# A decoder layer on one core: the rates at which feed forward is mixed into the attention, and the place of the weight roundings

## The chip, the core and the metric

The kernel runs on one core of a Trainium2 chip. Five engines work on it[...]: PE (matmul), VectorE (DVE), ScalarE (ACT), GpSimd (POOL) and SyncE (SP), which here only issues DMAs. The metric is the device time of one execution in microseconds; lower is better.

## The reference

One decoder layer with layer norms behind the residuals, for x of 2 x 1024 tokens x 256. Self attention has 16 heads of 16 with rotary tables and a causal mask; cross attention goes to 77 context tokens; the feed forward is gated, with two hidden layers of 1024 between.

```python
h = silu(tlin(x, w1_w, w1_s)) * tlin(x, w2_w, w2_s)      # 256 -> 1024
h = gelu(tlin(h, h1_w, h1_s))                            # 1024 -> 1024
h = gelu(tlin(h, h2_w, h2_s))                            # 1024 -> 1024
ffn = tlin(h, w3_w, w3_s)                                # 1024 -> 256
# tlin(x, w, s) = (x @ w.T) * s, w holds few distinct values
x = layernorm(x + attn(x, w_qkv, w_proj))                # causal, rotary
x = layernorm(x + xattn(x, ctx, ctx, mask, ...))         # 77 keys
x = layernorm(x + ffn(x))
```

## The kernel before

The 16 tiles of 128 tokens are taken in five chunks (`CHUNKS`): two chunks of two tiles, then three of four tiles. In the text they are chunks 0 to 4. For each chunk the attention goes through these stages:

- `start` (`project`): tokens are turned, queries, keys and values are projected (tiles `xT`, `pq`, `pv`, `qk_pad`), queries and keys are turned back into `q` and `kT`.
- `top` (`maxima`): for each query tile the scores of all four head groups are computed once, as one set of four or more small products into the two score banks `su` (`scores_bank`; there is one pair of them for everything), and VectorE reduces both banks to maxima (`part`, then `m`). The maxima are written into a spare row of `q`, by `sent` DMAs on SP or by a transposed add.
- `weighted` (`values`): the scores again, keys in the rows now, exponentials on ScalarE (`pr`; half of the tile goes through VectorE first), and products with the values (`po`).
- `rest`: `finish` (division, projection with `wproj`, residual and norm), `cross` (the same for the context, its maxima in `top` and `mx`, then its own `finish`), and for all but the first chunk `prepare`, which makes the two planes of the feed forward's input.

The feed forward of a chunk (`feed_forward_exact`) needs the end of that chunk's `rest`. It is 352 products on PE for a chunk of two tiles after its input is prepared, 384 for one of four tiles: `pg` and `pu` for the gate, `pf` for the two hidden layers, and `pf` again for w3. Its activations are gelu on ScalarE, and each hidden tile is split into an upper plane and a remainder (`split`, a subtract on VectorE or POOL). During `values` the gelus are put off (`behindhand`) until `catch_up`, so that the activation table need not change amid the exponentials.

The order of the work on PE, VectorE and ScalarE is the order of the program (`in_order`). It is made by generators. `beside` takes a step of attention; the number that the step yields is credit, in microseconds of PE that the feed forward may have before the next step; then as many feed-forward products are written as the credit pays for. When the feed forward of the chunks attended so far has run out, `starving[0]` is true, credit is dropped, and the stretch is dry. `together` mixes two generators of attention, `rest(n)` and the next chunk's `start` and `top`: it always takes a step of the one with the smallest sum of yields divided by pace (1.0 and 0.25).

POOL and SP are not bound to the program's order: the tile framework's scheduler places their instructions by their dependencies.

The hidden weights are read from DRAM in 22 slices of 128 x 1024 (`NS`). `survey` reads all of them once in the first part (`w`, `seen`) to find out whether they can be used exactly in one pass; `flag` chooses between two branches, and with these inputs it is the one with `feed_forward_exact`. For that branch each slice is copied from DRAM to DRAM by a DMA on POOL's queue, which rounds it (`rounded`); `half_slices` then loads half slices `wr` on SP's queue, six buffers deep, for every chunk anew. Eight of the roundings (`SOONER`) are issued by the survey's first eight steps, and the other fourteen at the head of the branch.

Of the kernel before, what the change touches and what calls it, by code (L numbers as in the profile page):

```python
# [31 lines left out]
KB = KT * P  # L32
# [3 lines left out]
NS = N12 + 2 * NH + N3  # L36
GATES = 3
SOONER = 8
# [5 lines left out]
def kernel(ctx: ExitStack, tc: tile.TileContext, a: dict, out: bass.AP):  # L44
# [107 lines left out]
    for n, (b, t0, nt) in enumerate(CHUNKS):  # L152
        for i in range(nt):
            xs[b, t0 + i] = residual[(0, 2, 4, 8, 0)[n] + i]

    def load_x(b, t):
        nc.sync.dma_start(xs[b, t], a["x"][b, t * P : (t + 1) * P, :])
# [317 lines left out]
    def maxima(b, t0, n, q):  # L475

        late = None
        for i in range(n):
            cols = slice(i * P, (i + 1) * P)
            spans = spans_of(t0 + i)  # L480
            part = pl.small.tile([P, len(spans), NG, 4], F32, tag="part", name="part", bufs=2)
            for m, (kk, c0, c1) in enumerate(spans):
                diagonal = m == len(spans) - 1
                r = c1 - c0
                gs = 512 // r
                for g0 in range(0, NG, gs):
                    gm = min(gs, NG - g0)
                    su = scores_bank()
                    calls = []
                    if diagonal:  # L490
                        for j in range(4):
                            to = su[j // 2][:, j % 2, :].rearrange("p (g n) -> p g n", g=NG)
                            turned_back = ident_h.unsqueeze(1).to_broadcast([P, NG, P])
                            calls.append(((to, causal[:, :P], turned_back), dict(start=True, stop=False)))
                    for gi in range(gm):
                        for j in range(4):
                            rows = slice(32 * j, 32 * j + 32)
                            calls.append(
                                (
                                    (  # L500
                                        su[j // 2][:, j % 2, gi * r : (gi + 1) * r],
                                        q[rows, g0 + gi, cols],
                                        kT[b, kk][rows, g0 + gi, c0:c1],
                                    ),
                                    dict(start=not diagonal, stop=(not diagonal or gi == gm - 1)),
                                )
                            )
                    tiled(calls)
                    if late and first_part[0]:
                        turned = turned_maxima(late[0])  # L510
                    elif late:
                        sent_maxima(q, *late)
                        late = None
                    largest(part[:, m, g0 : g0 + gm, :].rearrange("p g j -> p j g"), su, gm, r)
                    if late:
                        add_maxima(turned, q, late[1])
                        late = None
                    phase[0] = "maxima"
                    yield (0.8 if first_part[0] else 1.6 if starving[0] else 2.6) * gm * r / KB
            top = maxima_of_heads("m")  # L520
            dve.tensor_reduce(top, part.rearrange("p n g j -> p (g j) n"), AX.X, ALU.max)
            late = top, cols
            phase[0] = "maxima"
            yield 0.3 if i < n - 1 or first_part[0] else 1.6
        add_maxima(turned_maxima(late[0]), q, late[1])
        yield 0.8 if first_part[0] else 1.2
# [152 lines left out]
            nc.sync.dma_start(t, a["wf"][i])  # L679
            yield t  # L680

    def half_slices():

        for i in range(2 * NS):
            t = pl.wffn.tile([P, SLICE // 2], F32R, tag="wr", name="wr")
            half = rounded[i // 2][:, i % 2 * (SLICE // 2) : (i % 2 + 1) * (SLICE // 2)]
            nc.sync.dma_start(t.bitcast(F32), half.bitcast(F32))
            yield t
# [181 lines left out]
        yield 1.0  # L870

    def feed_forward_exact(b, t0, n, alone):
        slices = half_slices()
        N = n * P
        product[0] = step = 0.23 * n / KT
        if (b, t0) not in prepared:
            yield from prepare(b, t0, n)
        planes = prepared[b, t0]

        def layer(name):  # L880
            t = pl.acts.tile([P, 2, FC, N], F32R, tag=name, name=name)
            return SimpleNamespace(planes=(t[:, 0], t[:, 1]), done=set())

        def of_units(w):
            return lambda p, k: (w[k // per][:, k % per, :], now.planes[p][:, k, :])

        now = layer("hid")
        raw = None
        for f in range(FC):
            w = next(slices).rearrange("p (s k n) -> p s k n", s=2, k=KC)  # L890
            pg, pu = (bank(name)[:, :N] for name in ("pg", "pu"))
            sums = [
                (ps, lambda p, k, s=s, w=w: (w[:, s, k, :], planes[p][:, k, :])) for s, ps in ((0, pg), (1, pu))
            ]
            for group in [sums] if f == 0 else [[x] for x in sums]:
                yield from planes_summed(group, KC, step, 0)
            before, raw = raw, gated(pg, pu, None, f)
            if f:
                split(before, now, f - 1)
            if f == 1 and behind_gate:  # L900
                behind_gate.pop()()
        split(raw, now, FC - 1)
        early, per = 6, FC // 2
        for s in (2, 3):
            nxt = layer("hid" if s == 3 else "mid")
            for f0 in (0, 2, 3, 4, 5, 6, 7):
                fs = (0, 1) if f0 == 0 else (f0,)
                sums = []
                for f in fs:
                    w = [next(slices).rearrange("p (k n) -> p k n", k=per) for _ in range(2)]  # L910
                    sums.append((bank("pf")[:, :N], of_units(w)))
                yield from planes_summed(sums, FC, step, early if f0 == 0 else 0, now.done)
                for f, (pf, _) in zip(fs, sums):
                    activated(pf, nxt, s, f)
            now = nxt
        through.add((b, t0))
        w3 = [next(slices).rearrange("p (k n) -> p k n", n=C) for _ in range(2 * N3)]
        mv = pl.small.tile([P, n, 2], F32, tag="mv", name="mv")

        def of_tokens(i):  # L920
            cols = slice(i * P, (i + 1) * P)
            return lambda p, k: (now.planes[p][:, k, cols], w3[k // 2][:, k % 2, :])

        for i0 in (0, *range(2, n)):
            tiles = (0, 1) if i0 == 0 else (i0,)
            sums = [(bank("pf")[:, :C], of_tokens(i)) for i in tiles]
            yield from planes_summed(sums, FC, 0.12, early if i0 == 0 else 0, now.done)
            for i, (pf, _) in zip(tiles, sums):
                summed(pf, xs[b, t0 + i], mv[:, i, :])
                if alone:  # L930
                    written(b, t0 + i, 1, mv[:, i : i + 1, :])
        if not alone:
            behind_gate.append(lambda: written(b, t0, n, mv))

    def survey(flag):

        with ExitStack() as first:
# [11 lines left out]
            for i in range(4):  # L949
                load_slice(i)  # L950
            for i in range(NS):
                if i < SOONER:
                    nc.gpsimd.dma_start(rounded[i], a["wf"][i])
                w = loaded[i]
                low = w.bitcast(U16).rearrange("p (n two) -> p n two", two=2)[..., 0]
                if phase[0] == "values":
# [21 lines left out]
    def together(*streams):  # L978

        live = [[g, pace, 0.0] for g, pace in streams]  # L980
        while live:
            s = min(live, key=lambda s: s[2] / s[1])
            try:
                step = next(s[0])
                s[2] += step
                yield step
            except StopIteration:
                live.remove(s)
# [40 lines left out]
    def weighted(n):  # L1029
        if n == 3:  # L1030

            assert {(0, 0), (0, 2)} <= written_out
            load(4)
        yield from values(*CHUNKS[n], queries_of(n))
# [46 lines left out]
        qk_pads.pop()  # L1081
    other_weights = nc.values_load(flag, min_val=0, max_val=1)

    def beside_each_other(forward, wbufs):
        starving[0] = True
        attended.clear()
        attended.add(0)
        written_out.clear()
        exactly[0] = forward is feed_forward_exact
        if exactly[0]:  # L1090
            for i in range(SOONER, NS):
                nc.gpsimd.dma_start(rounded[i], a["wf"][i])
        with part() as mine, in_order():
            pl.wffn = mine.enter_context(tc.tile_pool(name="wffn", bufs=wbufs))
            pl.acts = mine.enter_context(tc.tile_pool(name="acts", bufs=1))
            last = len(CHUNKS) - 1
            parts = [top(1)]
            for n in range(1, last):
                parts += [weighted(n), together((rest(n), 1.0), (chain(start(n + 1), top(n + 1)), 0.25))]
            parts += [weighted(last), rest(last)]  # L1100
            run(beside(chain(*parts), chain(*(fed(n, forward) for n in range(last + 1)))))

# [88 lines left out]
```

## Time and profile before

| what | value |
|---|---|
| median of 3 runs | 1044.72 us (1041.94 to 1045.3) |
| the profiled execution | 1038.93 us, span 1037.2 us |
| mean granted PE clock | 0.944 |
| busy: PE, DVE, ACT, POOL | 916.3, 546.6, 425.8, 174.7 us |
| DMA | 89.61 MB, mean 86 GB/s |
| ACT table loads | 25, 1283 ns each |
| VectorE reductions of scores, 128 x 1024 | 1215 to 1220 ns each |

The profile is of one execution. "Busy" is the time in which an engine has an instruction in hand; the tenths of the page's part 2 give it for 40 equal slices of the span, some 26 us each. The granted clock is the share of full speed that PE was given. In an engine's rows an `x8` counts records; an fp32 product leaves two records, a product of rounded operands one. Some records of matmuls can be missing.

### The profile page before, as it was taken

The page shows a single profiled execution, that of the slowest core. Times are in us where ns is not written, and L with a number is a line of the kernel's source. Part 1 is how long each engine was busy: PE and PEld are TensorE (multiplying, and loading weights), DVE is VectorE, ACT ScalarE, POOL GpSimd, SP SyncE. Part 2 cuts the span into 40 slices and gives each one's busy share as a digit, 9 for nine tenths or more (in the row PEclk, how much of TensorE's full clock was granted, in tenths as well). Part 3 has the DMA queues.
Part 4 walks back from the last instruction along what each step waited for, and adds up shares of the span by engine and source line. Part 5 has one row for each costly group of instructions (what it writes and reads, how often), then busy time and mean ns, then how long its engine had stood idle before and what let it go on. Part 6 is the DMA issues. An engine that isn't in the chain of part 4 may idle for free.

```text
span 1037.2 us, 16399 instructions
## 1 busy us (share of the span) xinstructions
PE 916.3 (88%) x6537; PEld 560.7 (54%) x6542; DVE 546.6 (53%) x887; ACT 425.8 (41%) x668; POOL 174.7 (17%) x257
## 2 busy tenths in 40 slices
PE   7587688998999888999999978889999998778995
PEld 4344574775774644566642365356664326426884
DVE  4364534446645646865555455676665546356213
ACT  2364237333348114332278821423225783144431
POOL 5020421111321200231210102023221100100001
PEclk9788879899999999899999999989999999778998
DMA  8862861230541200222310010012221001002441
GB/s 271 264 227 99 277 192 61 92 113 22 172 154 42 82 3 1 72 92 82 102 42 21 11 49 5 1 50 93 93 92 61 21 11 36 18 0 92 142 146 52
DMA packets 45109, 89.61 MB, mean 86 GB/s; under 512 B 7128, under 2 KB 12928, under 8 KB 44672
## 3 DMA queue, kind: packets, MB, share of 16 engines
q1 hardware_dynamic: 44047, 76.15, 22.8%
q0 software_dynamic: 704, 11.54, 3.3%
q8 instruction: 54, 0.88, 0.4%
q10 hardware_dynamic: 272, 0.79, 0.2%
q14 instruction: 32, 0.25, 0.1%
HBM read 86.19 MB, written 13.63 MB: 96 GB/s over the span
## 4 chain that ended last, share of the span: by engine, by line
PE 68%; DVE 14%; ACT 5%; issue 2%; DMA 2%; POOL 1%; POOLq 0%; DVEq 0%; ACTq 0%
PE pf L89 25%; PE su L89 20%; PE po L89 6%; PE pm L89 5%; PE pt L89 4%; DVE pr L89 3%; PE pg L89 3%; PE pu L89 3%; ACT pr L89 3%; DVE x L89 2%; DMA wr<-rounded 2%; PE pq L89 2%; DVE top L89 2%; DVE stats L89 1%; DVE part L89 1%
## 5 line engine op out<-in xcount | busy, mean ns | idle before, releaser
L89 DVE TENSOR_REDUCE part<-su 128x2 f32<-128x1024 f32 (+3 forms) x149 | 166.8, 1160 | 93.9 <-PE su L89 93.8
L89 PE MATMUL pf<-mid,wr 128*128 128x512 f32 (+1 forms) x640 | 148.8, 369 | 0.5 <-DVE x L89 0.5
L89 PEld LDWEIGHTS pf<-mid,wr 128*128 128x128 f32 x640 | 105.3, 191 | 57.2 <-issue 41.7
L89 PE MATMUL pf<-hid,wr 128*128 128x512 f32 (+1 forms) x640 | 131.7, 357 | 1.2 <-DVE gate L89 1.2
L89 ACT ACTIVATE raw<-pf,sc 128x512 f32<-128x512 f32 (+1 forms) x71 | 42.3, 606 | 190.4 <-PE pf L89 188.9
L89 PEld LDWEIGHTS pf<-hid,wr 128*128 128x128 f32 x640 | 103.7, 192 | 30.7 <-issue 12.3
L89 ACT ACTIVATE pr<-su 128x1024 f32<-128x1024 f32 (+1 forms) x124 | 96.3, 776 | 53.7 <-PE su L89 50.2
L89 ACT ACTIVATE pr<-pr 128x1024 f32<-128x1024 f32 (+1 forms) x124 | 100.2, 808 | 19.4 <-DVE pr L89 14.8
L89 PE MATMUL su<-q,kT 32*128 32x512 f32 (+3 forms) x832 | 94.8, 514 | 5.4 <-ACT pr L89 4.8
L89 PE MATMUL su<-kT,q 32*128 32x128 f32 (+3 forms) x1152 | 92.2, 416 | 1.6 <-DVE part L89 1.6
L89 PE MATMUL po<-pr,v 128*32 128x512 f32 (+3 forms) x832 | 87.4, 482 | 5.4 <-ACT pr L89 3.2
L89 DVE TENSOR_TENSOR pr<-su,causal 128x512 f32<-128x512 f32 (+1 forms) x64 | 48.5, 757 | 57.4 <-PE su L89 46.2
L89 DVE COPY pr<-su 128x1024 f32<-128x1024 f32 (+1 forms) x40 | 44.7, 1118 | 44.3 <-PE su L89 43.0
L588 POOL TENSOR_SCALAR_AFFINE_SELECT pr<-pr 128x256 f32<-128x256 f32 x64 | 26.5, 414 | 212.9 <-ACT pr L89 212.9
L89 PEld LDWEIGHTS su<-q,kT 32*128 32x128 f32 x832 | 35.0, 186 | 46.4 <-ACT pr L89 41.6
L89 PEld LDWEIGHTS su<-kT,q 32*128 32x128 f32 x1152 | 44.7, 189 | 28.3 <-issue 16.0
L89 PE MATMUL pg<-x,wr 128*128 128x512 f32 (+1 forms) x160 | 45.5, 397 | 8.4 <-DMA wr<-rounded 7.1
L89 PEld LDWEIGHTS po<-pr,v 128*32 128x32 f32 x832 | 18.1, 109 | 60.1 <-ACT pr L89 28.3
L263 POOL TENSOR_SCALAR rstd<-mv 128x4 f32<-128x4 f32 (+2 forms) x18 | 4.0, 231 | 276.0 <-DVE mv L89 276.0
L89 ACT ACTIVATE gate<-pg,sc 128x512 f32<-128x512 f32 (+1 forms) x40 | 24.0, 602 | 58.3 <-PE pg L89 56.4
L89 ACT ACT_TABLE_LOAD x25 | 32.1, 1283 | 36.2 <-PE su L89 26.9
L788 POOL TENSOR_TENSOR mid<-raw,mid 128x512 fp32r<-128x512 f32 (+1 forms) x29 | 29.7, 1033 | 100.0 <-ACT mid L89 97.7
(131 smaller groups left out, 1233.7 us busy)
## 6 DMA issues: line engine op xcount, KB each, us to landing
wr<-rounded SPq DMA_DIRECT2D x220, 256.0 KB
rounded<-in_wf_dram POOLq DMA_DIRECT2D x22, 512.0 KB, 11.3
w<-in_wf_dram SPq DMA_DIRECT2D x22, 512.0 KB
x<-in_x_dram SPq DMA_DIRECT2D x16, 128.0 KB
out_dram<-x SPq DMA_DIRECT2D x16, 128.0 KB
q<-sent SPq DMA_DIRECT2D x80, 2.0 KB
wqkv<-in_w_qkv_dram ACTq DMA_DIRECT2D x1, 768.0 KB
wk<-in_wkT_dram SPq DMA_DIRECT2D x1, 512.0 KB
```

The source lines that it names most:

```text
L89: ins = getattr(self.engine, name)(*args, **kw).ins
L263: nc.gpsimd.tensor_scalar(rstd, mv[:, :, 1], EPS, None, ALU.add)
L588: nc.gpsimd.affine_select(out=half, in_=half, compare_op=ALU.is_ge, fill=0.0, base=0, pattern=[[0, 2], [1, P]], channel_multiplier=-1,)
L788: sub.tensor_tensor(rest, raw, upper.bitcast(F32), ALU.subtract)
```

## The change

Four edits in the generators:

- In `maxima`, the credit of a step is 1.7 for a full step in all chunks but the first part, where it was 2.6 with feed forward at hand and 1.6 without.
- In `together`, a pace is a function that is asked at each step, and a stream's sum is of yields divided by the pace at that moment. The pace of the next chunk's `start` and `top` is 0.6 while the feed forward has run out and 0.25 otherwise.
- In the survey, the first eight roundings are issued in the last eight steps, not the first eight.
- The other fourteen are issued in `half_slices` of the first chunk's feed forward, one before every second half slice, eight slices ahead of it, and no longer at the head of the branch.

```diff
+    def round_slice(i):
+        nc.gpsimd.dma_start(rounded[i], a["wf"][i])
...
     def maxima(b, t0, n, q):
-                    yield (0.8 if first_part[0] else 1.6 if starving[0] else 2.6) * gm * r / KB
+                    yield (0.8 if first_part[0] else 1.7) * gm * r / KB
...
-    def half_slices():
+    def half_slices(rounding):
         for i in range(2 * NS):
+            if rounding and i % 2 == 0 and i // 2 + SOONER < NS:
+                round_slice(i // 2 + SOONER)
             t = pl.wffn.tile([P, SLICE // 2], F32R, tag="wr", name="wr")
...
     def feed_forward_exact(b, t0, n, alone):
-        slices = half_slices()
+        slices = half_slices((b, t0) == CHUNKS[0][:2])
...
     def survey(flag):
             for i in range(NS):
-                if i < SOONER:
-                    nc.gpsimd.dma_start(rounded[i], a["wf"][i])
+                if i >= NS - SOONER:
+                    round_slice(i - (NS - SOONER))
...
     def together(*streams):
         while live:
-            s = min(live, key=lambda s: s[2] / s[1])
+            s = min(live, key=lambda s: s[2])
             try:
                 step = next(s[0])
-                s[2] += step
+                s[2] += step / s[1]()
                 yield step
...
+    def beside_rest():
+        return 0.6 if starving[0] else 0.25
+
     def beside_each_other(forward, wbufs):
-        if exactly[0]:
-            for i in range(SOONER, NS):
-                nc.gpsimd.dma_start(rounded[i], a["wf"][i])
...
-                parts += [weighted(n), together((rest(n), 1.0), (chain(start(n + 1), top(n + 1)), 0.25))]
+                parts += [weighted(n), together((rest(n), lambda: 1.0), (chain(start(n + 1), top(n + 1)), beside_rest))]
```

## The prediction

> **What bounds the kernel now.** I read the page first, then busy time by stage (the windows view, cut at the stage borders that the PE timeline shows), then the timeline of one step in the stages that change.
>
> The page's parts 1 and 2 come first: busy time and share of each engine, and the span in 40 slices.
>
> ```profile
> PE 916.3 (88%) x6537; PEld 560.7 (54%) x6542; DVE 546.6 (53%) x887; ACT 425.8 (41%) x668; POOL 174.7 (17%) x257
> PE   7587688998999888999999978889999998778995
> PEclk9788879899999999899999999989999999778998
> ```
>
> PE is the bound, with 121 us of idle (1037.2 - 916.3). The dips in slices 13 to 15, 24 to 26 and 34 to 36 recur, and the clock dips with two of them. The windows view says where they are (stretch: length, busy time and record count of PE, PEld, DVE, ACT, POOL, then clock).
>
> ```profile
> 357.00:425.50 68.50, 57.72 (x382) 30.11 (x384) 40.74 (x78) 20.34 (x29) 8.79 (x11) 0.93 0.01 1
> 430.00:530.00 100.00, 99.39 (x643) 63.15 (x639) 62.21 (x66) 31.31 (x46) 26.35 (x21) 1.00 0.29 96
> 594.50:619.50 25.00, 20.87 (x129) 16.89 (x126) 14.64 (x39) 6.99 (x15) 1.35 (x2) 1.00 0.06 19
> 619.50:686.50 67.00, 55.12 (x375) 28.73 (x375) 40.38 (x80) 19.69 (x28) 10.33 (x13) 0.95 0.05 14
> 690.00:795.50 105.50, 104.89 (x671) 66.32 (x670) 67.21 (x73) 32.60 (x48) 26.92 (x21) 1.00 0.29 96
> 860.00:879.80 19.80, 16.80 (x107) 14.07 (x107) 12.17 (x34) 5.40 (x11) 1.27 (x2) 1.00 0.07 21
> 879.80:941.90 62.10, 45.54 (x295) 22.57 (x296) 28.66 (x64) 14.31 (x18) 5.50 (x8) 0.78 0.05 16
> ```
>
> 430:530 and 690:795.5 are the maxima of chunks 3 and 4, beside feed forward: PE has no idle time at all. 357:425.5, 619.5:686.5 and 879.8:941.9 are the cross attentions of chunks 2, 3 and 4 after the feed forward has run dry: 10.8 + 11.9 + 16.6 us idle, and in the last a clock of 0.78. So feed forward is spent where PE was full anyway, and missing where PE waits. One step of the maxima (timeline, chunk 4) says how much room those stages have on the other engines.
>
> ```profile
> 732.64 1.14 PE L89 MATMUL su<-kT,q 32*128 32x512 f32 x8
> 733.71 2.79 PE L89 MATMUL pf<-hid,wr 128*128 128x512 f32 x11
> 733.82 2.35 DVE L89 TENSOR_REDUCE part<-su 128x2 f32<-128x1024 f32 x2 [1.70 <-PE su L89]
> ...
> 736.43 1.14 PE L89 MATMUL su<-kT,q 32*128 32x512 f32 x8
> ```
>
> A step is 3.79 us: scores 1.07, eleven products 2.72 (0.247 each). VectorE reads both score banks for 2.35 us and is through at 736.17, 0.26 us before PE writes them again. There is one pair of score banks, so this is all the slack the maxima have.
>
> **The change, part by part.** Counting feed-forward products in the order of both programs, stage by stage (maxima / values / finish, cross and the next chunk's start):
> chunk 1: 158/45/149 before, 112/45/195 after; chunk 2: 250/37/65, then 166/37/149; chunk 3: 284/36/64, then 163/37/184; chunk 4: 284/36/64, then 187/36/161. The total is the same. The tail (the last chunk's feed forward, 941.9 to 1037.2) is untouched. Prices: 0.247 us at 512 columns (chunks 3, 4), 0.13 at 256 (chunks 1, 2: 17 in 2.2 us), 0.123 for w3 (64 in 7.83 us).
>
> Maxima of chunk 4: 97 products leave, 24.0 us. But with 7.4 products (1.83 us) a step asks 2.90 us of PE, while the banks are busy 1.07 + 2.35 = 3.42. PE can refill the first bank while VectorE reads the second, so the step lies between 2.90 (nothing lost) and 3.45 (nothing overlapped). Following two steps by hand, every second one finds its second bank 0.5 us late: I take 3.15, 0.25 above PE's own time, over some 22 steps 6 us. Behind such a wait on PE stand the next products, and behind those ScalarE's and POOL's activations, which have room (32.60 and 26.92 of 105.50 busy). The gate layer adds a VectorE multiply (741 ns) per eight products to steps that already need 2.35: 3 us. The slow start at 683 to 690 (slow clock, 4 us) goes. Sum -24 + 6 + 3 - 4 = -19.
>
> Maxima of chunk 3: 121 products leave (-29.9), five score sets move into chunk 2's dry stretch (-6), waits as above over 17 steps +5, gate +3: -28.
>
> Maxima of chunk 2: 84 products, -10.9, one set moves out -2, new waits +1: -12. Maxima of chunk 1: 46 products, -6.
>
> Finish and cross of chunk 4 (860 to 941.9, 81.9 us): PE's own work at full clock is 16.8 + 45.5 x 0.78 = 52.3, of which 64 w3 products are 8. After: 44.3 + 97 x 0.247 + 64 x 0.123 = 76.1, plus 6 us of waits that stay (16.80 of 19.80 busy in 860:879.8, which had feed forward beside it): 82. So 24 us of products go in for nothing: 0. The cover is VectorE's and ScalarE's latency in this chain and the clock; should it fail, the 24 us come back. The `wr` loads on SP move with their products, into stretches where the DMA engines are 0.05 busy.
>
> Chunk 3 (594.5 to 686.5, 92 us): 20.9 + 55.1 x 0.95 = 73.3, less 8, plus 120 x 0.247 + 64 x 0.123 = 37.5, plus one more set 1.1, plus waits 6: 110, +18.
>
> Chunk 2 (335 to 425.5, 90.5): its products still run out, after the second of four cross maxima. 84 products come in (+10.5), of which some 5 are hidden. The faster pace puts seven score sets of chunk 3 where there were two. They use the same banks and 2.4 us of VectorE each, in the queue of the chain that ends the stretch (its `x` waits are the longest): two us each, +10. Sum +15.5.
>
> Chunk 1's cross: +46 products (5.8), hidden in the 6.5 us idle of 230 to 253 but for 2; one set more, +1.5.
>
> ScalarE: 24 table loads in this branch become 31; 17 subtracts go from POOL (1.28 us) to VectorE (0.69). What matters are round trips inside the values, where a feed-forward layer ends amid exponentials: one before, in chunk 1, three after, in chunks 2, 3 and 4. The one in the trace:
>
> ```profile
> 176.10 1.28 ACT L89 ACT_TABLE_LOAD   x1
> 177.39 1.03 ACT L89 ACTIVATE raw<-raw 128x256 f32<-128x256 f32 x3
> 178.44 1.28 ACT L89 ACT_TABLE_LOAD   x1
> ```
>
> cost PE 2.97 us waiting for `pr`. The Trainium skill ("ScalarE: Activation LUTs", What ACT_TABLE_LOAD costs) speaks against the change here: it gives a switch about 1283 ns for the load and 1380 more for a drain. By the row the activation starts 10 ns after the load's end and the next load as soon after it: no drain. By the row the three trips cost 9 us and the one that goes gives 3: +6. By the page two more switches' drains per trip make it about +11. I take the row; the page stays in the range.
>
> The roundings: the text moves them, the order hardly does. POOL isn't bound to the program's order, and the eight early ones stand in both programs right after the memsets, waiting for nothing: they still start near 11 us (9.5 before), in the first load of the DMA queues. Of the fourteen later ones eleven still stand in a row at the branch; only the last three are each behind one `hid` subtract. So the burst stays that stalls PE for 7.1 us on `wr` near 124 and 131. The subtracts come some 4 us sooner on POOL, freeing gate buffers; one score set more passes before the stall. I take -2, between 0 and -8; were a late rounding to hold SP's queue, `sent` and the weights behind it would wait, but eight slices' lead leaves that at +3 at most.
>
> Sum: -19 - 28 - 12 - 6 + 0 + 18 + 15.5 + 3.5 + 6 - 2 = -24. The profiled execution took 1038.9 us (span 1037.2), 0.6% under the median, 1044.7; -24 makes 1015 of it and 1020 of the median.
>
> **The rivals.**
> (a) Gain as worked out, 1020: chance 0.58.
> (b) The score banks cost less and the cross hides more. For: in chunk 1's cross, with feed forward beside it, PE idles under 1 us from 197 to 231. Without the bank waits (-12), the new gate waits (-3) and the round trips (-6): -45, 1000. Chance 0.16.
> (c) The banks bind fully: 3.45 a step is +0.3 over 40 steps, 12 us, and VectorE's additional work some 5: -8, about 1037. Chance 0.16, a third of it close enough to zero to be called no change.
> (d) Slower: feed forward beside the cross is not hidden but added. Its activations and subtracts stand in order on ScalarE and VectorE ahead of the small operations that the chain waits for (`y`, `x`, `top`). If nothing is hidden, chunk 4 pays 24 instead of 0, chunk 3 30 instead of 18, chunks 1 and 2 9 more: 44 in all, 1064. It turns the sign where less than about 45% is hidden. Against it stands chunk 1's cross, but with half as wide tiles. Chance 0.10.
> (e) The rounding edit does nothing at all: within (a), 2 us.
>
> **How the numbers follow.** Faster by over 0.3% (3 us, about what a measurement of this kernel can tell from no change): (a), (b), two thirds of (c): 0.84. Within: 0.06. Slower: 0.10. The range leaves out (d) and the far end of (b): 998 to 1041.
>
> **What would show it.** Right: no step of the maxima near 3.79 us, but steps of about 2.9 to 3.4 with PE waiting for `part`; PE over 90% busy and the clock near 1 in the cross of chunks 3 and 4; a dry stretch left in chunk 2 alone, ended by VectorE; 32 table loads in the page; PE idle near 105 us. Wrong: the maxima of chunks 3 and 4 shorter by under 30 us together, or the stages of cross 3 and 4 longer by over 40.

## The result and the profile after

| | before | after |
|---|---|---|
| median (range, 4 runs each) | 1043.33 us (1037.93 to 1045.3) | 1058.07 us (1055.06 to 1059.9) |
| ratio, 95% interval | | 1.0147 (1.01 to 1.0193) |
| profiled span | 1037.2 us | 1056.7 us |

The change makes the kernel 1.5% slower; forecast was 2.4% faster. The page of the changed kernel, parts 1 and 2:

```profile
PE 941.8 (89%) x6542; PEld 564.7 (53%) x6542; DVE 555.1 (53%) x905; ACT 433.5 (41%) x671; POOL 160.9 (15%) x244
PE   7587799997989977799999899989999999988995
PEclk9788899999998988799999999988999999999998
```

PE's idle time fell only from 121 to 114.9 us, and its busy time rose by 25 us though it computes the same products. "Busy" contains products at half clock and sets that stand half written while their second bank is being read. The clock's dip in slices 35 to 37 (counted from one) is gone, as forecast. New ones are in slices 15 to 17 and 27 to 28. The stretches of the prediction again, in the windows view (325.5 to 440.9 is chunk 2's finish, cross and dry part; then the maxima of 3, a window that overlaps the first; finish and cross of 3; the maxima of 4; finish and cross of 4 in three pieces):

```profile
325.50:440.90 115.40, 94.74 (x628) 58.85 (x627) 60.43 (x123) 30.18 (x53) 11.36 (x14) 0.91 0.14 45
434.20:526.40 92.20, 90.02 (x525) 49.65 (x525) 65.59 (x73) 27.35 (x37) 17.26 (x14) 0.93 0.21 67
594.50:705.30 110.80, 100.90 (x608) 64.08 (x609) 54.46 (x119) 33.21 (x52) 14.66 (x16) 0.99 0.15 48
709.30:810.60 101.30, 96.95 (x569) 55.24 (x569) 68.93 (x74) 27.51 (x38) 20.10 (x16) 0.93 0.21 69
878.40:898.20 19.80, 19.14 (x93) 14.13 (x94) 12.31 (x31) 7.16 (x13) 2.60 (x4) 1.00 0.25 80
898.20:954.30 56.10, 51.76 (x375) 31.26 (x375) 25.40 (x51) 19.52 (x25) 5.15 (x6) 1.00 0.12 39
954.30:960.60 6.30, 5.17 (x35) 4.00 (x33) 4.58 (x15) 1.18 (x2) 1.27 (x2) 1.00 0.49 158
```

Finish and cross of 3 take 110.8 us against 110 forecast. Those of 4 are filled at full clock and take 82.2 us against 82 forecast, with 76.07 us of PE against 76.1. But chunk 2's stretch and the maxima of 3 together, 325.5 to 526.4, take 200.9 us; before they took 195 (335 to 530), and 182.5 was forecast. Cross 3 and the maxima of 4 together, 594.5 to 810.6, take 216.1 us; before 201, and 200 was forecast.

To compare kernels I cut each trace at VectorE events that all of them have: the last `m` of a chunk ends its maxima, the last `q<-po` its values, the last `rec` its cross ("maxima" of chunks 2 to 4 therefore hold the end of `rest` and the next start as well, and the tail holds the end of the last `rest`). First column: us before; then the forecast's steps, and the difference to before in each profiled execution. The last column is the changed kernel with the old pace beside chunk 2 alone (`pace_not_chunk_2` below).

| stage | before | forecast | after | credit 1.7 alone | pace alone | credit 2.2, new pace | 1.7, old pace beside 2 |
|---|---|---|---|---|---|---|---|
| first part | 101.0 | 0 | -1.2 | +0.5 | +1.6 | -0.7 | -1.9 |
| maxima 1 | 50.3 | -8 | -8.4 | -8.4 | -1.5 | -4.1 | -8.1 |
| values 1 | 34.2 | -3 | -5.0 | -5.0 | +0.7 | -4.5 | -5.0 |
| cross 1 | 55.8 | +3.5 | -0.8 | -0.8 | +2.2 | +0.2 | -0.8 |
| maxima 2 | 58.0 | -12 | +1.0 | +0.3 | -1.4 | -4.4 | +1.0 |
| values 2 | 34.6 | +3 | +3.8 | +3.4 | +0.2 | -0.3 | +3.8 |
| cross 2 | 76.6 | +15.5 | +26.0 | +8.8 | +18.2 | +15.0 | +12.5 |
| maxima 3 | 109.6 | -28 | -19.1 | -8.6 | -12.1 | -15.3 | -11.7 |
| values 3 | 75.2 | +3 | +3.6 | -0.7 | +0.4 | -0.5 | -0.7 |
| cross 3 | 79.7 | +18 | +18.9 | +8.6 | +9.5 | +13.8 | +8.7 |
| maxima 4 | 110.5 | -19 | -3.7 | -11.3 | -5.0 | -12.2 | -13.6 |
| values 4 | 75.1 | +3 | +3.3 | -0.5 | -0.1 | -0.3 | +3.4 |
| cross 4 | 73.0 | 0 | -4.9 | +0.8 | -2.3 | -3.4 | +0.2 |
| tail | 103.5 | 0 | +6.0 | +2.6 | -0.8 | -0.7 | +7.2 |
| span | 1037.2 | -24 | +19.5 | -10.1 | +9.6 | -17.3 | -5.0 |

How far a stage repeats: the changed kernel was profiled twice (the second is `credit_22_late` below), and no stage differs by more than 2.1 us between the two, those from cross 3 to the tail by 0.3 at most.

### The profile page after: what moved, and what is told of

It is laid out like the page before. It is cut to its first block, busy times and chain, and to the rows that moved or that the text cites. A ratio compares the mean times of both kernels' runs of the same rounds, so it can differ in the third digit from the quotient of the medians.

```text
span 1056.7 us, 16404 instructions
## 1 busy us (share of the span) xinstructions
PE 941.8 (89%) x6542; PEld 564.7 (53%) x6542; DVE 555.1 (53%) x905; ACT 433.5 (41%) x671; POOL 160.9 (15%) x244
## 4 chain that ended last, share of the span: by engine, by line
PE 69%; DVE 13%; ACT 5%; issue 3%; DMA 2%; POOL 1%; SPq 0%; POOLq 0%; DVEq 0%; ACTq 0%
PE pf L89 23%; PE su L89 21%; PE po L89 6%; PE pm L89 5%; PE pt L89 5%; ACT pr L89 3%; DVE pr L89 3%; PE pg L89 3%; PE pu L89 3%; DVE part L89 2%; DVE x L89 2%; PE pq L89 2%; DMA wr<-rounded 1%; PE pv L89 1%; DVE stats L89 1%
## 5 line engine op out<-in xcount | busy, mean ns | idle before, releaser
L89 DVE TENSOR_REDUCE part<-su 128x2 f32<-128x1024 f32 (+3 forms) x149 | 166.9, 1160 | 75.1 <-PE su L89 74.7
L89 PE MATMUL pf<-mid,wr 128*128 128x512 f32 (+1 forms) x640 | 168.3, 387 | 1.7 <-PE pf L89 1.0
L89 PE MATMUL pf<-hid,wr 128*128 128x512 f32 (+1 forms) x640 | 141.3, 361 | 0.1
L89 PE MATMUL su<-kT,q 32*128 32x128 f32 (+3 forms) x1152 | 115.0, 432 | 6.4 <-DVE part L89 6.4
L89 PE MATMUL su<-q,kT 32*128 32x512 f32 (+3 forms) x832 | 96.1, 521 | 11.4 <-ACT pr L89 10.7
L89 PEld LDWEIGHTS su<-kT,q 32*128 32x128 f32 x1152 | 53.5, 195 | 46.8 <-issue 26.9
L793 POOL TENSOR_TENSOR hid<-gate,hid 128x256 fp32r<-128x256 f32 (+1 forms) x32 | 32.8, 1028 | 108.4 <-ACT hid L89 108.4
```

Of the source, the lines that this page charges most:

```text
L89: ins = getattr(self.engine, name)(*args, **kw).ins
L793: sub.tensor_tensor(rest, raw, upper.bitcast(F32), ALU.subtract)
```

## The experiments

Every time below is a median; ratios are to the kernel before, run beside it on the same chip.

**The parts alone.** `credit_only` is the hunk of `maxima` on the kernel before, `pace_only` the hunks of the paces (`together`, `beside_rest` and its call), `roundings_only` the rest.

> The kernel before with one part of the change, the credit of 1.7 in the maxima; paces and roundings as before. Theory of the score banks: a step of the maxima cannot go under about 3.45 us (scores 1.07 and both reductions 2.35), so of the products taken out of chunks 3 and 4 only those above that length save time; the rest cost their full time in the cross stages. Then this part alone carries most of the loss: 1048 to 1058 us, with the steps of the maxima of chunk 4 at 3.4 to 3.5 us. Rival, the pace edit is the cause (seven score sets in chunk 2's dry stretch): then the credit alone is worth what was forecast for it, 1015 to 1035 us.

> The kernel before with another part alone, the pace of 0.6 for the next chunk where feed forward is dry. Theory of the score banks: the early score sets lengthen the dry cross of chunks 2 and 3, and each comes out of the maxima at its full step: within 8 us of the kernel before, 1036 to 1052. Rival, the pace edit is the cause: 1053 to 1070 us, the dry stretches of chunks 2 and 3 longer by 10 us or more each than the maxima behind them become shorter.

> The kernel before with only the weight roundings placed as in the change. Both theories, and the order of the instructions: the early eight start with the others in the first load, eleven of the other fourteen stand together at the branch, so 1041 to 1046 us, no change. Rival: the late roundings hold the loads of wr, 1048 us or more, with longer waits of PE for wr between 110 and 160 us.

| run | us | ratio (95%) |
|---|---|---|
| credit_only | 1027.59 | 0.9852 (0.9827 to 0.9876) |
| pace_only | 1048.57 | 1.0051 (1.0028 to 1.0075) |
| roundings_only | 1042.18 | 1.0005 (0.9988 to 1.0021) |

The first theory falls: the credit alone gains 14 us, as its rival said. The roundings do nothing. But the pace alone costs only 7, which was the first theory's answer for it. -14, +7 and 0 make -7; together the parts make +15. Some 22 us belong to neither part, only to the pair. In the stage table the pair's part is "after" less both single columns: next to nothing in cross 2 (-1.0) and cross 3 (+0.8), and +12.6 in maxima 4, +3.9 each in values 3 and 4, +4.2 in the tail, -3.4 in cross 4.

**Another credit.** In the changed kernel 1.7 becomes 2.2, then also 2.0 and 2.4; and 2.2 with the old paces.

```diff
-                    yield (0.8 if first_part[0] else 1.7) * gm * r / KB
+                    yield (0.8 if first_part[0] else 2.2) * gm * r / KB
```

> The changed kernel with a credit of 2.2 in place of 1.7, all else as changed. Theory of the score banks: 9.5 products of 0.247 us and the scores, 1.07, make 3.4 us, just what the banks take anyway, so the maxima of chunks 3 and 4 are as long as with 1.7 (within 3 us each), some 40 products a chunk leave the cross stages, and the total falls by 10 to 16 us to 1042 to 1048. Rival (maxima are bound by PE alone, products cost the same everywhere): each step longer by 0.5 us, maxima of chunks 3 and 4 longer by 8 us each, cross shorter by as much, total within 4 us of the changed kernel, 1054 to 1062.

> The changed kernel with a credit of 2.0 in all maxima. Between 1.7 (1058) and 2.2 (1024). Theory of the overflow: it depends on whether products still stand behind the last cross; 2.0 is 1.3 products a step more than 1.7 over some 20 steps, 26 of the 37 that spill into the tail, so 1026 to 1040. Rival (a smooth optimum of the mixing rate, without a spill): near 1036, halfway on a line.

> The changed kernel with a credit of 2.4. Theory of the score banks: above 2.2 a product costs its full 0.247 us in the maxima again, about 0.9 products a step over some 40 steps of chunks 3 and 4, 9 us, less what the cross gives back: 1026 to 1036. If the gates and waits bind before, 2.4 is no worse than 2.2 (1020 to 1026), and this is the better version.

> The kernel before with a credit of 2.2 alone. Theory of the overflow: with 2.2 no backlog spills, with the new pace or the old, so the pace is worth no more than 5 us here: 1019 to 1029 us (1024 with the new pace). Rival (the pace edit costs its 7 us in any company, as it did on the kernel before): 1015 to 1019 us.

| run | us | ratio (95%) |
|---|---|---|
| credit_20 | 1029.11 | 0.9879 (0.9829 to 0.9929) |
| credit_22 | 1023.96 | 0.9827 (0.9786 to 0.9868) |
| credit_24 | 1034.6 | 0.9916 (0.9879 to 0.9953) |
| credit_22_old_pace | 1029.6 | 0.9876 (0.983 to 0.9923) |

credit_22 beats both kernels; against credit_only and credit_20 the intervals overlap. Both expectations for it missed: 1042 to 1048 and 1054 to 1062. 0.3 us of credit a step, from 1.7 to 2.0, is worth 29 us beside the new pace. With the old paces 1.7 and 2.2 are level (1027.59 and 1029.6, the intervals overlap). So 1.7 isn't past an edge by itself, only beside the new pace; and at 2.2 the new pace costs nothing that can be told (the intervals overlap, the medians even favour it). The page of credit_22:

```profile
PE 914.6 (90%) x6536; PEld 558.3 (55%) x6542; DVE 552.7 (54%) x899; ACT 423.4 (42%) x667; POOL 162.7 (16%) x245
PEclk9698989999999998999999999889999999999998
```

27 us less PE time than in the changed kernel for the same products. Its maxima of chunk 4 (second line) hold 217 feed-forward products by my count, those of the changed kernel (first line) 195, and yet they are 8.5 us shorter, at a clock of 0.97 for 0.92:

```profile
693.83:800.72 106.89, 100.95 (x581) 58.40 (x581) 76.37 (x96) 22.46 (x35) 20.71 (x18) 0.92 0.20 67
```

```profile
674.26:772.61 98.35, 95.01 (x592) 58.26 (x591) 70.43 (x86) 24.38 (x37) 23.44 (x20) 0.97 0.22 73
```

**The score banks.** One step of the maxima of chunk 4 at a credit of 1.7, in the timeline of credit_only:

```profile
745.05 1.86 PE L89 MATMUL pf<-hid,wr 128*128 128x512 f32 x7
745.54 2.33 DVE L89 TENSOR_REDUCE part<-su 128x2 f32<-128x1024 f32 x2
...
746.89 2.26 PE L89 MATMUL su<-kT,q 32*128 32x512 f32 x8
...
748.06 2.36 DVE L89 TENSOR_REDUCE part<-su 128x2 f32<-128x1024 f32 x2 [0.18 <-PE su L89]
749.08 1.88 PE L89 MATMUL pf<-hid,wr 128*128 128x512 f32 x7
750.89 1.14 PE L89 MATMUL su<-kT,q 32*128 32x512 f32 x8
```

The set at 746.89 takes 2.26 us, the next one 1.14. VectorE reads until 745.54 + 2.33 = 747.87; the second half of the set can only start then. The view calls PE busy all this time. From set to set the four full steps of this tile (sets at 743.72, 746.89, 750.89, 754.00 and 757.37) take 3.17, 4.00, 3.11 and 3.37 us, 3.41 in the mean. If VectorE sets this, half as long reductions must show it:

```diff
-        dve.tensor_reduce(to[:, :2], first, AX.X, ALU.max)
-        dve.tensor_reduce(to[:, 2:], other, AX.X, ALU.max)
+        few = r if first_part[0] else r // 2
+        dve.tensor_reduce(to[:, :2], first[..., :few], AX.X, ALU.max)
+        dve.tensor_reduce(to[:, 2:], other[..., :few], AX.X, ALU.max)
```

> The kernel before with the credit of 1.7, and each reduction of scores reads only the first half of its keys (half of the maxima's work on VectorE is left out). Theory of the score banks: at 7.4 products the step (mean 3.4 us) waits for the banks, so with reductions half as long it falls to PE's own 2.9, and the maxima of chunks 3 and 4 (101.0 and 99.2 us) become 8 to 12 us shorter each. Rival (what keeps the steps long is on PE itself): they stay within 3 us.

> The kernel before, credit 2.6, with the same half reductions (half of the maxima's work on VectorE is left out). Theory of the score banks: at 11 products PE is the bound, so the maxima of chunks 3 and 4 (109.6 and 110.5 us) stay within 4 us. Rival (VectorE bounds these steps at either credit): 8 us or more shorter each.

Of both there is one run, 994.14 and 1019.83 us. With credit 1.7 the maxima of 3 and 4 went from 101.0 and 99.2 to 87.4 and 89.0 us, and the step that waited is gone (timeline of credit_only_half_max, 2.88 us from set to set):

```profile
723.72 1.14 PE L89 MATMUL su<-kT,q 32*128 32x512 f32 x8
724.79 1.88 PE L89 MATMUL pf<-hid,wr 128*128 128x512 f32 x7
724.92 1.29 DVE L89 TENSOR_REDUCE part<-su 128x2 f32<-128x512 f32 x2 [1.84 <-PE su L89]
726.60 0.93 PE L89 MATMUL su<-kT,q 32*128 32x384 f32 x8
```

With 2.6 they went from 109.6 and 110.5 to 104.1 and 105.3. That is over the 4 us expected, but the full steps stayed where they were, 3.79 us from set to set with eleven products (timeline of before_half_max):

```profile
713.43 1.14 PE L89 MATMUL su<-kT,q 32*128 32x512 f32 x8
714.50 2.79 PE L89 MATMUL pf<-hid,wr 128*128 128x512 f32 x11
714.60 1.29 DVE L89 TENSOR_REDUCE part<-su 128x2 f32<-128x512 f32 x2 [2.11 <-PE su L89]
717.22 1.14 PE L89 MATMUL su<-kT,q 32*128 32x512 f32 x8
```

About half of its gain lies in the first steps of each maxima, before feed forward is there (2.9 of 5.5 us in chunk 3, 2.5 of 5.2 in chunk 4). The same four full steps in every kernel, by the starts of their sets; "PE's own" is 1.07 us of scores and 0.247 a product:

| kernel | credit | products in four steps | PE's own, us a step | measured, us a step |
|---|---|---|---|---|
| before | 2.6 | 45 | 3.85 | 3.92 |
| before, half reductions | 2.6 | 45 | 3.85 | 3.85 |
| credit_24 | 2.4 | 41 | 3.60 | 3.74 |
| credit_22 | 2.2 | 39 | 3.48 | 3.64 |
| credit_20 | 2.0 | 35 | 3.23 | 3.59 |
| credit_only | 1.7 | 29 | 2.86 | 3.41 |
| after | 1.7 | 30 | 2.92 | 3.54 |
| credit_only, half reductions | 1.7 | 29 | 2.86 | 2.97 |

So a step is PE-bound at 2.6, and at 1.7 it is held up by VectorE. Between them there is no sharp floor: from 45 to 29 products PE is asked for 0.99 us a step less, and the step becomes 0.51 shorter. About half of what is taken out is saved in the maxima, and all of it must be placed elsewhere.

**Which chunks, which pace.** First, 2.2 in chunks 3 and 4 alone. The run credit_22_late compared a pair of numbers with triples, so it was the changed kernel once more: 1062.01 us, which says how far a repeat goes (1058.07 the first time). credit_22_chunks_3_4 is the edit as meant.

```diff
-                    yield (0.8 if first_part[0] else 1.7) * gm * r / KB
+                    yield (0.8 if first_part[0] else 2.2 if (b, t0, n) in CHUNKS[3:] else 1.7) * gm * r / KB
```

> The changed kernel with a credit of 2.2 in the maxima of chunks 3 and 4 alone, 1.7 in those of chunks 1 and 2. Theory of the overflow: what spills past cross 3 and cross 4 goes (16 and 37 products), the maxima of chunk 3 and 4 stay within 4 us of the changed kernel's or shorter, so most of the loss to the 2.2 kernel comes back: 1026 to 1036 us. Rival (the loss starts in chunks 1 and 2 by their spill into chunk 2's start): 1045 us or more.

> The changed kernel with a credit of 2.2 in the maxima of chunks 3 and 4, 1.7 in those of chunks 1 and 2. Theory: the spill past cross 3 and cross 4 is decided in the maxima of chunks 3 and 4, so it goes, with the trips in their values: 1028 to 1038 us. Rival (the backlog starts in chunks 1 and 2, whose spill into the start of chunk 2 sets the rest): 1045 us or more.

1034.25 us, ratio 0.9899 (0.9863 to 0.9934): of the 34 us between the changed kernel and credit_22, the credit of chunks 3 and 4 brings 24, and that of chunks 1 and 2 the other 10. Then the pace back at 0.25 beside the rest of one chunk:

```diff
-                ... (chain(start(n + 1), top(n + 1)), beside_rest))]
+                ... (chain(start(n + 1), top(n + 1)), (lambda: 0.25) if n == 2 else beside_rest))]
```

> The changed kernel (credit 1.7), with the pace of the next chunk back at 0.25 beside the rest of chunk 2 alone; beside chunks 1 and 3 it is the changed one. Theory of the overflow: the score sets of chunk 3 that pass in chunk 2's dry cross bring no feed forward with them, since credit is dropped while it is dry; 30 products fewer in the maxima of chunk 3, and the backlog spills past cross 3, into the start of chunk 4 and the tail. Then this one edit undoes the interaction: 1026 to 1034 us, no product of chunk 2's feed forward behind cross 3, maxima of chunk 4 near 99 us (107 in the changed kernel). Rival (each early set costs by itself, wherever it is placed, and chunk 3's stay): half of the loss or less comes back, 1042 us or more.

> The changed kernel with the pace back at 0.25 beside the rest of chunk 1 alone. Theory: feed forward hardly runs dry there with a credit of 1.7, so the new pace does little: 1050 to 1060 us. Rival (chunk 1's pace holds the 11 us that the kernel with the old pace beside chunk 2 still lacks to the credit alone): 1044 to 1049 us.

Beside chunk 2: 1038.56 us, 0.9961 (0.9941 to 0.9981), with single runs from 1033.8 to 1044.1. It is between the two expectations: some 20 of 30 us. Its profile is of one of its fastest runs, 1033.89. Beside chunk 1: 1057.95, nothing. So the pair meets in chunk 2's cross: with the new pace the maxima of chunk 3 hold 24 sets, not 26, and 156 products, not 186. A set that passes while it is dry takes its credit along. The dry stretch, from the last product before it to the first behind it, in the windows view (the changed kernel, then pace_not_chunk_2):

```profile
373.50:444.10 70.60, 52.55 (x321) 24.62 (x320) 44.06 (x78) 15.84 (x21) 4.78 (x6) 0.85 0.02 8
```

```profile
373.10:425.00 51.90, 40.47 (x259) 20.17 (x259) 33.98 (x68) 15.83 (x21) 4.79 (x6) 0.90 0.02 7
```

It begins at the same time (373.5 and 373.1) and holds 6.5 sets against 2.5 (by the reductions in it); at seven or eight products a set, the four more are the 30 that are missing. They lengthen it by 18.7 us. The loss of the pair shows behind it: with the old pace there, values 3 gets back 4.3 us and maxima 4 gets back 9.9.

**Table trips.** In the changed kernel's values a layer of the feed forward ends amid exponentials three times. ScalarE's timeline and PE's, chunk 4:

```profile
806.73 1.28 ACT L89 ACT_TABLE_LOAD   x1
808.02 0.63 ACT L89 ACTIVATE raw<-raw 128x512 f32<-128x512 f32 x1
808.67 1.28 ACT L89 ACT_TABLE_LOAD   x1
809.97 1.02 ACT L89 ACTIVATE pr<-su 128x1024 f32<-128x1024 f32 x1
```

```profile
811.04 1.61 PE L89 MATMUL su<-q,kT 32*128 32x512 f32 x8 [2.61 <-ACT pr L89]
```

```diff
         for layer, f, raw in tiles:
-            act.activation(raw, raw, AF.Gelu)
+            if phase[0] == "values":
+                act.activation(raw, raw, AF.Exp, scale=0.0)
+            else:
+                act.activation(raw, raw, AF.Gelu)
```

> The changed kernel; where put-off gelus are caught up amid exponentials, an exponential of zero is computed in their place (those gelus are left out), so no table is changed there. Theory: each of the three trips in the values costs 3.3 to 4 us of PE's time, so 8 to 13 us go, to 1045 to 1050 us, and the rest of the loss stays in the maxima and the cross. Rival (the trips cause most of the loss): 1038 us or less; other rival (their time is covered): 1055 or more.

1049.16 us, ratio 1.006 (1.004 to 1.008): 9 us less than the changed kernel at first, and 12.9 less than its copy that ran beside this one (credit_22_late, 1062.01). Values 2, 3 and 4 became 4.4, 4.2 and 4.2 us shorter, 12.8 in all. So the trips are 9 to 13 of the 34 us. In chunk 4 the wait is 2.61 of the 4.2; behind it PE runs at half clock from 811.6 to 815.0, which loses 1.7 more, and without the trip it doesn't.

**The spill.** In the changed kernel the feed forward of chunk 3 isn't through when cross 4 ends. PE's timeline there:

```profile
954.31 3.21 PE L89 MATMUL pf<-wr,hid 128*128 128x256 f32 x24
957.80 1.96 PE L89 MATMUL pt<-ident,x 128*128 128x128 f32 x8 [0.28 <-DVE x L89]
```

By my count 37 products stand behind the last `rec`, and 16 behind cross 3. I thought these were the edge that 2.0 avoids. To test it, 64 products are left out, in the changed kernel and in credit_22, where nothing spills:

```diff
-            yield from planes_summed(sums, FC, 0.12, early if i0 == 0 else 0, now.done)
+            yield from planes_summed(sums, FC, 0.12, early if i0 == 0 else 0, now.done, 1 if n == 4 and not alone else 2)
```

(The new last argument is the number of planes, two where it isn't given.)

> The changed kernel; in the feed forward of chunks 2 and 3 the second plane of the w3 products is left out, 32 products each, 64 x 0.123 = 7.9 us of PE's time in all. In the changed kernel 16 and 37 products spill past cross 3 and cross 4. Theory of the spill: without it the maxima of chunk 4 and the tail give back 5 us each beyond the products' own time, 1040 to 1047 us in all. Rival (products cost their own time wherever they are): 1049 to 1052 us.

> The kernel with credit 2.2 and the new pace, and the same 64 products left out; nothing spills there. Theory of the spill: they cost no more than their own time, and part of it is hidden beside the cross, so 3 to 8 us go: 1016 to 1021. Rival (leaving out w3 products shortens a chain of its own): 1013 or less.

1055.49 us, 1.0137 (1.0092 to 1.0182), and 1022.92, 0.9812 (0.978 to 0.9845): 3 and 1 us less, each time less than either expectation had. The theory falls. In the profile the tail gave back 3.3 us for 32 products (3.9 us at 0.123) and the maxima of chunk 4 only 1.8. Spilled products cost at most their own time.

## Why the prediction was wrong

The order of the work was read rightly: by count, 184 products are written from the end of values 3 to the end of that feed forward (168 up to the last `rec`, 16 behind it) and 161 in chunk 4 (124 and 37), as forecast, and 32 tables are loaded. Several stages came out too: cross 3 (+18, measured +18.9), and cross 4 and the last feed forward. The stage table cuts these two at the last `rec` (-4.9 and +6.0); at the forecast's own border, the first gate product of the last feed forward, they are 82.2 us for 82 and 96.1 for 95.3. The forecast's own sign of being wrong held: the maxima of 3 and 4 became 22.8 us shorter together, under 30.

Two sums came out in part by luck. Chunk 1's maxima (-8, -8.4) had 2 us of the roundings in them; `roundings_only` shows +0.1 there, and the credit alone has the -8.4. The trips (+6; three at 3.3 to 3.8 and one fewer at -5.0 make +5.7) were priced at 3 each. The prediction's row showed the loads rightly, with no drain between them, but PE's wait isn't the whole price: a trip takes 4.2 to 4.4 us of its stage.

The sum missed by 43.5 us, from -24 to +19.5. By stage: maxima 4 by 15.3, maxima 2 by 13.0, cross 2 by 10.5, maxima 3 by 8.9. These steps failed:

- **"Two us each, +10."** The largest. Four more early score sets in chunk 2's dry cross made it 18.7 us longer, 4.7 each (the dry stretch of the changed kernel against that with the old pace there). 5.7 of that is half-clock time, 10.8 us against 5.1, which the forecast didn't have; the rest is still over 3 us a set. Taking the new pace away beside chunk 2 alone gives 19.5 us back.
- **"I take 3.15, 0.25 above PE's own time."** With credit alone the quiet step is 3.41, 0.55 above PE's own 2.86; in the changed kernel it is 3.54 (3.47 in chunk 3), over the forecast's upper end of 3.45. The half reductions show the mechanism: 2.97. For 40 steps this is 10 to 15 us. Rival (c) took the full binding but kept the rest of the sum. It doesn't turn the sign by itself: credit_only has it and gains 14 us.
- **Maxima 2, -12, measured +1.0.** Missed: with cross 1 no longer dry, w3 products of chunk 0 follow its end (18 by count), and PE then waits 3.94 us for `qk_pad` at 241 us, where it waited 2.01 before. With 2.2 nothing follows, the wait is 1.21, and the stage gains 4.4. The 18 products are worth 2.2 us at 0.123, PE's idle time in the stage rises by 2.6 and its half-clock time by 1.7. The rest of the 13 us isn't accounted for, and nothing was left out to test it.
- **Maxima 4, -19, measured -3.7.** Credit alone has -11.3. The other 7.6 us stand beside a clock that is lower by nearly as much (half-clock time lost: 8.5 us, against 1.7 in credit_only). VectorE comes into its first steps with the norm of the previous feed forward, and PE, with fewer products in hand, waits:

```profile
721.91 2.35 DVE L89 TENSOR_SCALAR x<-x,mv,rstd 128x256 f32<-128x256 f32 x4
...
724.38 2.33 DVE L89 TENSOR_REDUCE part<-su 128x2 f32<-128x1024 f32 x2
```

```profile
725.73 3.21 PE L89 MATMUL su<-kT,q 32*128 32x512 f32 x8 [2.14 <-DVE part L89]
```

The norm alone doesn't explain it. In credit_only it stands among the first steps as well, and PE waits nearly as long, but the clock stays full:

```profile
696.38 2.32 DVE L89 TENSOR_SCALAR x<-x,mv,rstd 128x256 f32<-128x256 f32 x4
```

```profile
698.93 0.27 PE L89 MATMUL pt<-ident,m 128*16 128x128 f32 x1 [1.95 <-DVE m L89]
```

Rival (d) named almost the time, 1064, for the wrong reason: feed forward beside cross 3 and 4 was hidden as forecast.

What stays open is the pair's 22 us in full. The trips of values 3 and 4 are 8 of them, shown by leaving them out. Most of the rest is maxima 4, 12.6 us: it goes when the new pace beside chunk 2 goes, which is shown. Why it is that long is not: half clock is some 7 of it, and leaving out the 16 products that spill into it gave back only 1.8.

## What to carry to other kernels

Filler beside a stage isn't paid in full or not at all. Count what the slowest other engine needs per step (here 3.4 us, scores and two reductions on one pair of banks) and compare it with PE's own time at several rates: well above it most of a product that is taken out is saved, towards it less (here three quarters from 45 products to 39, under four tenths from 39 to 29), and all of it must be placed elsewhere. Edits that all move filler into one place must be tried together and apart, since each can gain or cost little alone and the pair lose: a credit of 1.7 was as good as 2.2 with the old paces and 34 us worse with the new one. And "PE busy" isn't PE computing: compare the duration of like sets (1.14 and 2.26 us) before believing that an engine is full.

## What the runs showed of the hardware

The granted clock comes in pieces of 3.41 us and multiples of it. I cut the trace into such pieces. In the changed kernel, 19 times a piece at full clock was followed by one at half: PE had been busy for 1 to 75% of the piece before, 33% in the mean; in pieces at full clock that were followed by full clock it was never under 54%. In the kernel before it was 15 times, 0 to 65%, and again 54%. Over all 18 traces the ranges overlap: up to 82% before half clock, down to 42% before full clock. The Trainium skill ("TensorE: Matmul & The Clock Gate", What's actually happening) gives the half rate for at least one idle window of about 3.4 us; here a wait of 2.14 us was enough. Windows view of the changed kernel around it:

```profile
716.00:723.00 7.00, 7.00 (x61) 4.41 (x61) 4.78 (x7) 1.74 (x4) 0.98 (x1) 1.00 0.25 77
723.00:726.00 3.00, 0.86 (x5) 0.46 (x5) 3.00 (x6) 0.90 (x2) 1.86 (x2) 1.00 0.52 175
726.00:733.00 7.00, 7.00 (x19) 3.23 (x20) 3.82 (x4) 1.19 (x2) 0.69 (x1) 0.52 0.12 40
733.00:740.00 7.00, 7.00 (x59) 4.21 (x53) 6.03 (x6) 2.07 (x4) 1.87 (x2) 0.99 0.23 76
```

After 2.14 us without a product PE runs for 7 us at 0.52: 3.4 us more are lost, in the clock column and not in any wait. The wait of 1.95 us in credit_only cost no clock:

```profile
697.00:699.00 2.00, 0.07 (x2) 0.10 (x2) 1.79 (x4) 0.11 (x1) 1.36 (x1) 1.00 0.85 300
699.00:706.00 7.00, 7.00 (x32) 3.56 (x31) 6.12 (x7) 2.60 (x4) 1.29 (x1) 1.00 0.18 61
```

The wait of 2.14 us lies within one piece (722.8 to 726.2), which is 37% busy; that of 1.95 us is split over two (they meet at 697.6), which are 81% and 62% busy. So a wait of 2 us on PE can cost over twice its length or only itself, and where it falls in the pieces goes with which. A stage can also begin at half clock after one that ended dry: in the changed kernel 436.1 to 449.8, behind chunk 2's dry cross, is at 0.50.
